# Moving SBUF-only products from VectorE to GpSimd in a two-layer codebook convolution

## The chip, the cores and the metric

The kernel runs on one core of one Trainium2 chip. The metric is the device time of one launch in microseconds, as the median of several runs. Engines are named as the profile does: PE is TensorE (PEld its weight loads), DVE is VectorE, ACT is ScalarE, POOL is GpSimd, and SP is SyncE, which here only issues DMAs.

## What is computed

The input `x` is 16 images of 256 channels, 28 x 28. Each is group-normalized (32 groups). Then come two layers of the same kind, a convolution through codebooks, and a closing gate:

```python
patches = 3x3 patches of each channel               # 9 values per channel and position
d       = |p|^2 - 2 p.centroids + |centroids|^2      # 16 centroids per channel
attn    = softmax(-d)
out     = sum over channels of attn @ (centroids @ w_sub)
# layer 1: relu(bn1(amm(gn(x)))) ; layer 2: bn2(amm(...))
s   = sigmoid(relu(mean(out) @ w1 + b1) @ w2 + b2)
x + relu(out * s + gn(x))
```

All of it is in 32-bit floats.

## The kernel before

**Blocks.** One image of one layer is four blocks: two halves of the channels (`hh`) by two halves of the rows (`t`, 14 x 28 = 392 positions), in the order `BLOCKS`. A block has nine *stacks*, tiles of 128 x 392: stack `k` holds, for its channels, the softmax-weighted part of patch row `k`. The list `KO` gives the order 8, 4, 5, 6, 7, 0, 1, 2, 3.

**How a stack is made.** `patches` (line 306 on, SyncE's queue) loads the 3x3 patches of the image from DRAM. `logits` (line 323, PE) writes eight PSUM banks per half block, `exps` (line 335, ACT) turns them into exponentials. `num_b` (line 384, PE) sums the denominators together with stack 8; `split_b` and `join_b` (lines 395 to 407, ACT and DVE) separate them, and `recip_dve` (line 410) inverts. `spread` (line 420, DVE) shuffles that reciprocal to the rows of a stack, into `rb`. `num_a` (line 370, PE) makes the numerators of stacks 0 to 7. Stacks 0 to 3 are copied out of PSUM unscaled by ACT (`copy_a`, line 430) and scaled later in SBUF by DVE (`scale_q`, line 424), as is stack 8; stacks 4 to 7 are scaled by DVE as they leave PSUM (`scale_a`, line 436).

**Seven products for eight.** The four blocks meet four weight matrices in a Strassen-like scheme. `PRODUCTS` lists eight calls of `product` (line 444, PE), numbered 5 to 12 by their slot: numbers 6 and 7 are the two parts of one product, 6 with the first four stacks of `KO`, 7 with the other five. Between them GpSimd forms differences of blocks, stack by stack, in place (`mix`, line 450). The results leave PSUM by `acc_copy` (ACT, line 466) and `acc_add` (DVE, lines 472 and 474), and two sums of regions by `reg_add` (line 479).

**Around the image.** In layer 0 the result, after batch norm and ReLU (`norm_out`, ACT, line 486), lies in the two tiles `hpads[0]` and `hpads[1]`, one per half of the output channels, which all images share. `to_home2` (line 499) scatters each with two indirect DMAs (r = 0 and 1) on GpSimd's queue into `home2[b]`; the second waits until the first has landed. The next image's input is normalized by `gn_apply` (line 291, GpSimd) and written to `home1` by `to_home1` (line 302, GpSimd's queue). For half of layer 1's blocks one group of logits is shifted by its maximum first (`wide_copy`, `wide_turn`, `wide_sub`, `wide_back`, `wide_exp`: DVE transposes, a reduction, a subtraction on line 355, and back); the subtraction runs on DVE for block 0 and on GpSimd for block 1. Layer 1 ends an image with `se_hidden`, `se_gate`, `finish_gate` (ACT), `finish_norm` (DVE, line 701), `finish_relu` (ACT), `finish_add` (GpSimd, line 707) and `store`.

**The order.** It is written out by hand. `at(slot, sub, f, ...)` files a call under a pair; at the end all calls are issued in the order of these pairs, and every engine runs its own in that order. An image begins every eight slots, so its slots 8 to 12 are slots 0 to 4 of the next. Even slots hold logits, `num_b`, `num_a` and a product, odd slots logits, `num_a` and a product. PSUM is a ring of eight banks, so an instruction that opens a bank waits for what read it eight banks ago; in each slot the eighth bank of the logits is the one of the product before. "Slot s" below is the slot modulo eight.

**Buffers.** The stacks live in a pool of `NQ` tiles that a small planner hands out by the slots of first and last use (`homes`, `LAST`).

## Time and profile before

| | us |
|---|---|
| median of 3 runs | 3113.1 (3111.44 to 3119.77) |
| profiled execution, its own time | 3117.03 |
| its span, first to last instruction | 3115.6 |
| PE busy in the span | 2845.3 |
| DVE busy | 2383.1 |
| POOL busy | 1643.0 |
| ACT busy | 1405.2 |
| mean granted clock of PE | 0.953 of full |

How to read the rows that follow. A row of the busy times by stretch holds: the stretch, its length, then busy us and (x instructions) of PE, PEld, DVE, ACT and POOL, the granted PE clock, the busy share of the DMA engines, and GB/s. A row of the timeline holds: start, length, engine, line, operation, out<-in names, shape, count, and in brackets how long the engine had been idle and what ended that. A row of the groups holds the count, total busy us, the mean ns of one, then idle time before them and what ended it. A row of one line's instructions holds min/median/max ns.

### The profile page before, as it was taken

The page shows a single profiled execution, that of the slowest core. Times are in us where ns is not written, and L with a number is a line of the kernel's source. Part 1 is how long each engine was busy: PE and PEld are TensorE (multiplying, and loading weights), DVE is VectorE, ACT ScalarE, POOL GpSimd, SP SyncE. Part 2 cuts the span into 40 slices and gives each one's busy share as a digit, 9 for nine tenths or more (in the row PEclk, how much of TensorE's full clock was granted, in tenths as well). Part 3 has the DMA queues.
Part 4 walks back from the last instruction along what each step waited for, and adds up shares of the span by engine and source line. Part 5 has one row for each costly group of instructions (what it writes and reads, how often), then busy time and mean ns, then how long its engine had stood idle before and what let it go on. Part 6 is the DMA issues. An engine that isn't in the chain of part 4 may idle for free.

```text
span 3115.6 us, 89074 instructions
## 1 busy us (share of the span) xinstructions
PE 2845.3 (91%) x37072; PEld 1313.2 (42%) x37072; DVE 2383.1 (76%) x4698; ACT 1405.2 (45%) x3216; POOL 1643.0 (53%) x1482
## 2 busy tenths in 40 slices
PE   6988999889999999899999999999999999999997
PEld 2333444434444444444444444444444444444444
DVE  5777677777767677676788887888888888788786
ACT  3434433433444434444344555454555454555443
POOL 4455456534655456554555544555554556454555
PEclk9999999999999999999999999999999999999999
DMA  9465555554555545555465344444444444444441
GB/s 230 91 123 148 159 141 147 126 144 101 128 142 138 128 100 128 142 138 126 92 141 138 82 108 107 105 101 105 93 103 108 99 109 98 105 91 109 103 103 46
DMA packets 211818, 368.10 MB, mean 118 GB/s; under 512 B 29432, under 2 KB 186472, under 8 KB 211408
## 3 DMA queue, kind: packets, MB, share of 16 engines
q1 hardware_dynamic: 199856, 300.39, 43.2%
...
q14 instruction: 114, 0.93, 0.1%
HBM read 284.78 MB, written 77.44 MB: 116 GB/s over the span
## 4 chain that ended last, share of the span: by engine, by line
PE 62%; DVE 28%; issue 3%; ACT 3%; DMA 2%; POOL 2%; SPq 0%; another core or an unknown queue 0%; DVEq 0%; POOLq 0%; ACTq 0%
PE acc L444 29%; PE lg L323 13%; PE nb L384 12%; DVE rb L420 7%; PE na L370 7%; DVE qs L424 6%; DVE r L410 5%; DVE y L701 2%; DVE qs L436 2%; ACT r L395 1%; DVE r L404 1%; DVE qs L407 1%; DVE hpad L472 1%; DMA home<-hpad,col 1%; POOL xpad L291 1%
## 5 line engine op out<-in xcount | busy, mean ns | idle before, releaser
L450 POOL TENSOR_TENSOR qs<-qs,qs 128x392 f32<-128x392 f32 x1152 | 1270.6, 1140 | 783.2 <-PE acc L444 621.6
L335 ACT ACTIVATE e<-lg 128x392 f32<-128x392 f32 x1920 | 782.1, 528 | 1051.1 <-PE lg L323 1049.0
L444 PE MATMUL acc<-qs,w_S 128*128 128x392 f32 x2304 | 822.1, 508 | 34.0 <-POOL qs L450 33.2
L323 PE MATMUL lg<-pt,wd 32*32 32x392 f32 x16384 | 637.6, 509 | 184.7 <-DVE hpad L472 85.1
L420 DVE STREAM_SHUFFLE rb<-r 128x392 f32<-128x392 f32 x1152 | 647.5, 595 | 0.0
L444 PEld LDWEIGHTS acc<-qs,w_S 128*128 128x128 f32 x2304 | 430.7, 193 | 428.3 <-POOL qs L450 85.0
L444 PE MATMUL acc<-qs,w_A 128*128 128x392 f32 x1728 | 595.5, 499 | 0.0
L424 DVE TENSOR_TENSOR qs<-qs,rb 128x392 f32<-128x392 f32 x640 | 537.3, 840 | 54.4 <-DVE rb L420 0.9
L323 PEld LDWEIGHTS lg<-pt,wd 32*32 32x32 f32 x16384 | 239.4, 104 | 510.8 <-issue 190.3
L444 PEld LDWEIGHTS acc<-qs,w_A 128*128 128x128 f32 x1728 | 321.5, 190 | 274.6 <-ACT e L335 39.6
L384 PE MATMUL nb<-e,cwb 64*32 64x392 f32 x8192 | 426.7, 557 | 0.2 <-issue 0.2
L370 PE MATMUL na<-e,cwa 64*32 64x392 f32 x8192 | 408.6, 497 | 14.0 <-DVE hpad L472 11.5
L404 DVE SCALAR_TENSOR_TENSOR r<-nb,kst,r 128x392 f32<-128x392 f32 x128 | 79.9, 624 | 414.0 <-ACT r L395 404.0
L410 DVE RECIPROCAL r<-r 128x392 f32<-128x392 f32 x128 | 331.9, 2593 | 0.0
L436 DVE TENSOR_TENSOR qs<-na,rb 128x392 f32<-128x392 f32 x512 | 252.7, 554 | 99.8 <-PE na L370 98.1
L384 PEld LDWEIGHTS nb<-e,cwb 64*32 64x32 f32 x8192 | 152.4, 118 | 268.8 <-issue 215.2
L499 POOL DMA_INDIRECT home<-hpad,col x60 | 60.4, 1006 | 370.2 <-ACT hpad L486 185.4
L370 PEld LDWEIGHTS na<-e,cwa 64*32 64x32 f32 x8192 | 143.7, 107 | 239.3 <-issue 111.1
L430 ACT COPY qs<-na 128x392 f32<-128x392 f32 x512 | 210.5, 505 | 12.9 <-PE na L370 12.7
L395 ACT ACTIVATE r<-nb,kst 128x392 f32<-128x392 f32 x128 | 86.7, 678 | 208.1 <-PE nb L384 186.0
L355 POOL TENSOR_TENSOR z<-z,mx 128x1568 f32<-128x1568 f32 x16 | 45.8, 2862 | 225.6 <-DVE mx L349 225.6
L341 ACT COPY e<-lg 128x392 f32<-128x392 f32 x128 | 52.9, 500 | 119.3 <-PE lg L323 119.3
...
## 6 DMA issues: line engine op xcount, KB each, us to landing
...
home<-xpad POOLq DMA_DIRECT2D x30, 899.0 KB, 7.0
...
home<-xpad SPq DMA_DIRECT2D x2, 899.0 KB
...
```

The lines of the kernel that those rows point to most:

```text
L323: nc.tensor.matmul(bk[32 * c : 32 * c + 32, :N].rearrange("p (r w) -> p r w", w=W), lhsT=wts["wd", u["hh"]][32 * i : 32 * i + 32, mm, c, : ...
L335: nc.scalar.activation(eg[:, i, :], bk[:, :N], AF.Exp, scale=2.0)
L370: nc.tensor.matmul(bs[r][32 * i : 32 * i + 32, :N], lhsT=wts["cwa", u["hh"]][64 * r : 64 * r + 64, mm, i, :], rhs=es[64 * r : 64 * r + 64, ...
L384: nc.tensor.matmul(bs[r][32 * i : 32 * i + 32, :N], lhsT=wts["cwb", u["hh"]][64 * r : 64 * r + 64, mm, i, :], rhs=es[64 * r : 64 * r + 64, ...
L395: nc.scalar.activation(r, b0[:, :N], AF.Identity, bias=zero, scale=m_hi)
L410: nc.vector.reciprocal(u["r"], u["r"])
L420: nc.vector.stream_shuffle(rb, u["r"], mask_of(k))
L424: nc.vector.tensor_mul(u["q", k], u["q", k], u.pop(("rb", k)))
L430: nc.scalar.copy(u["q", k], bk[:, :N])
L436: nc.vector.tensor_mul(u["q", k], bk[:, :N], u.pop(("rb", k)))
L444: nc.tensor.matmul(accs[key][:, :N], lhsT=wl[w][:, k, :], rhs=us["q", k], start=first and n == 0, stop=last and n == len(ks) - 1,)
L450: nc.gpsimd.tensor_tensor(out_u["q", k], in0["q", k], in1["q", k], ALU.subtract)
```

## The change

- **Pairs.** Stacks 0 to 7 are kept as pairs, tiles of 128 x 2 x 392 (14 of them), stack 8 in four single tiles. `mix` takes a pair in one instruction: five per difference instead of nine. `rb` is shuffled into pairs too, with one buffer of its own for stack 8.
- **Scaling.** `scale_q` moves from DVE to GpSimd: two pairs and one single per block.
- **Differences.** The second difference of layer 1 moves from slot 7, sub 2.6, to slot 8, sub 1.9. Product 6 takes three stacks and product 7 six.
- **Norm.** `gn_apply` moves to ACT, one slot later (slot 5, 0.9), and `to_home1` to SyncE's queue (slot 5, 1.9).
- **Scatters.** The four indirect DMAs of an image are filed at (12, 0.5), (12, 2.9), (13, 2.4) and (14, 2.9), one by one; before, they stood two and two at (12, 0.5) and (13, 0.5).
- **Sums.** The second `reg_add` moves from DVE to GpSimd and an `acc_add` more on DVE goes with it. All wide subtractions run on GpSimd.
- **Closing.** `finish_gate` and a `finish_norm` with a result of its own run on ACT in slot 14 (before: slot 15), `se_gate` ahead of `num_b`; a new `finish_sum` adds the two on GpSimd (on DVE for the last image); ReLU, add and store move up by half a slot to a slot.
- **Constants.** A mask of 512 columns becomes a row of 256 numbers and a comparison.

```diff
-NQ = 33
+NQ = {"pair": 14, "one": 4}
-    5: ("A11", 0, KO), 6: ("S1", 0, KO[:4]), 7: ("S1", 0, KO[4:]), 8: ("S3", 1, KO), 9: ("S4", 2, KO),
+    5: ("A11", 0, KO), 6: ("S1", 0, KO[:3]), 7: ("S1", 0, KO[3:]), 8: ("S3", 1, KO), 9: ("S4", 2, KO),
...
+    def gn_apply(b, k):
+        nc.scalar.activation(
+            grid(xpads[k])[:, 1 : H + 1, 1 : W + 1], xs[b][:, k].rearrange("p (r w) -> p r w", w=W), AF.Identity,
+            bias=nrm[:, b, 2, k : k + 1], scale=nrm[:, b, 1, k : k + 1],
+        )
...
+            rb = rpool.tile([P, 2, N], F32, tag="rb", name="rb", bufs=4)
+            for r in range(2):
+                nc.vector.stream_shuffle(rb[:, r, :], u["r"], mask_of(2 * mm + r))
...
-    def scale_q(u, k):
-        nc.vector.tensor_mul(u["q", k], u["q", k], u.pop(("rb", k)))
+    def scale_q(u, mm):
+        q = u["q", 8] if mm == 4 else pair(u, mm)
+        nc.gpsimd.tensor_tensor(q, q, u.pop(("rb", mm)), ALU.mult)
...
+            nc.gpsimd.tensor_tensor(pair(out_u, mm), pair(in0, mm), pair(in1, mm), ALU.subtract)
...
     def finish_gate(b, k):
-        nc.scalar.activation(y, y, AF.Identity, bias=nrm[:, b, 2, k : k + 1], scale=se[b][:, k : k + 1])
+        nc.scalar.activation(y, y, AF.Copy, scale=se[b][:, k : k + 1])
     def finish_norm(b, k):
-        nc.vector.scalar_tensor_tensor(y, xs[b][:, k], nrm[:, b, 1, k : k + 1], y, op0=ALU.mult, op1=ALU.add)
+        if k == 0:
+            ys[b, "t"] = io.tile([P, 1568], F32, tag="pb", name="xn")
+        nc.scalar.activation(
+            ys[b, "t"][:, HW * k : HW * k + HW], xs[b][:, k], AF.Identity,
+            bias=nrm[:, b, 2, k : k + 1], scale=nrm[:, b, 1, k : k + 1],
+        )
+    def finish_sum(b, k, eng):
+        eng.tensor_tensor(ys[b, k], ys[b, k], ys[b, "t"][:, HW * k : HW * k + HW], ALU.add)
...
+            for mm in (4, 2, 3, 0, 1):
+                at(g + 5, 2.5, mix, us[0], mm, us[1], us[0])
+                at(g + 7, 2.5, mix, us[1], mm, us[2], us[1])
+                at(g + (7 if l == 0 else 8), 2.6 if l == 0 else 1.9, mix, us[0], mm, us[2], us[0])
+                at(g + 10, 2.5, mix, us[0], mm, us[0], us[3])
...
-            at(g + 11, 0.02, reg_add, l, b, (1, 1), (1, 1), (1, 0), nc.vector)
+            at(g + 10, 0.05, reg_add, l, b, (1, 1), (1, 1), (1, 0), nc.gpsimd)
+            at(g + 11, 0.01, acc_add, l, b, 1, 1, (n, 10), pop=False)
+            at(g + 11, 0.02, acc_add, l, b, 0, 1, (n, 10))
...
-                        at(g + 12 + o, 0.5, to_home2, b, o)
+                        for r in range(2):
+                            at(g + 12 + o + (o and r), (0.5, 2.9)[r] if o == 0 else (2.4, 2.9)[r], to_home2, b, o, r)
...
-                        at(g + 4 if b else 3, 2.0 + 0.1 * q, gn_apply, b + 1, q)
-                        at(g + 4 if b else 3, 2.01 + 0.1 * q, to_home1, b + 1, q)
+                        at(g + 5 if b else 3, 0.9, gn_apply, b + 1, q)
+                        at(g + 5 if b else 3, 1.9, to_home1, b + 1, q)
...
-                at(g + 14, 2.1, se_gate, b)
+                at(g + 14, 1.05, se_gate, b)
                 for q in range(NB):
-                    at(g + 15, 0.9 + 0.01 * q, finish_gate, b, q)
-                    at(g + 15, 1.9 + 0.01 * q, finish_norm, b, q)
+                    at(g + 14, 1.9, finish_gate, b, q)
+                    at(g + 14, 1.91, finish_norm, b, q)
                     if b < B - 1:
-                        at(g + 16, 0.9, finish_relu, b, q)
-                        at(g + 16, 1.0, finish_add, b, q)
-                        at(g + 17, 0.6, store, b, q)
+                        at(g + 15, 0.5, finish_sum, b, q, nc.gpsimd)
+                        at(g + 15, 1.9, finish_relu, b, q)
+                        at(g + 16, 0.05, finish_add, b, q)
+                        at(g + 16, 2.9, store, b, q)
```

148 lines of the change are left out of this document (72 added, 76 removed).

## The prediction

> **What bounds the kernel now.** I read the page first (busy times, then the chain), then the busy time of each engine stretch by stretch, then the timeline of two images.
>
> ```profile
> PE 2845.3 (91%) x37072; PEld 1313.2 (42%) x37072; DVE 2383.1 (76%) x4698; ACT 1405.2 (45%) x3216; POOL 1643.0 (53%) x1482
> PE 62%; DVE 28%; issue 3%; ACT 3%; DMA 2%; POOL 2%; SPq 0%; another core or an unknown queue 0%; DVEq 0%; POOLq 0%; ACTq 0%
> ```
>
> TensorE is busy 91% of the time, yet the chain runs through VectorE for 28%. So TensorE stops for VectorE somewhere, and at most 270 us (3115.6 - 2845.3) of idle time is to be had, plus what a cold clock costs. The next two views locate it. Each row is one slot of the schedule. The first eight are one image of layer 0, slots 2, 3, 4, 5, 6, 7, 0, 1; the second eight are the same slots in layer 1.
>
> ```profile
> 840.64:853.54 12.90, 12.90 (x179) 6.00 (x178) 8.27 (x16) 6.00 (x14) 5.11 (x5) 1.00 0.35 76
> 853.54:864.28 10.74, 10.32 (x115) 4.80 (x115) 9.70 (x24) 4.41 (x10) 4.38 (x5) 1.00 0.42 91
> 864.28:877.88 13.60, 13.60 (x184) 6.58 (x183) 8.78 (x25) 6.59 (x15) 2.90 (x4) 1.00 0.47 126
> 877.88:887.52 9.64, 9.64 (x115) 4.74 (x114) 7.24 (x19) 3.81 (x9) 8.60 (x7) 1.00 0.66 201
> 887.52:900.53 13.01, 10.59 (x170) 4.79 (x169) 7.35 (x8) 6.49 (x15) 6.96 (x8) 0.87 0.73 231
> 900.53:907.48 6.95, 6.95 (x108) 3.17 (x107) 6.95 (x12) 3.72 (x9) 4.93 (x6) 1.00 0.48 94
> 907.48:927.71 20.23, 15.89 (x180) 6.43 (x179) 12.27 (x30) 6.12 (x14) 18.37 (x18) 0.83 0.46 104
> 927.71:937.36 9.65, 9.65 (x116) 4.75 (x115) 7.32 (x20) 3.23 (x8) 0.00 (x0) 1.00 0.48 102
> ```
>
> ```profile
> 2351.49:2363.68 12.19, 12.19 (x180) 5.94 (x179) 10.14 (x15) 6.01 (x14) 5.87 (x4) 1.00 0.63 180
> 2363.68:2374.45 10.77, 10.32 (x116) 4.77 (x115) 10.46 (x24) 5.99 (x13) 6.46 (x7) 1.00 0.42 91
> 2374.45:2387.20 12.75, 12.75 (x179) 5.99 (x178) 8.05 (x19) 6.68 (x16) 0.00 (x0) 1.00 0.36 77
> 2387.20:2397.13 9.93, 9.93 (x123) 5.01 (x122) 7.50 (x17) 3.90 (x10) 5.39 (x5) 1.00 0.49 99
> 2397.13:2406.56 9.43, 9.43 (x175) 4.55 (x173) 4.58 (x8) 6.62 (x16) 4.77 (x5) 1.00 0.47 106
> 2406.56:2413.57 7.01, 7.01 (x107) 3.23 (x106) 6.89 (x21) 5.85 (x13) 3.99 (x4) 1.00 0.48 101
> 2413.57:2433.93 20.36, 14.96 (x180) 6.18 (x179) 19.59 (x24) 7.62 (x16) 20.36 (x17) 0.83 0.28 62
> 2433.93:2443.96 10.03, 10.03 (x116) 4.77 (x115) 9.51 (x23) 4.61 (x9) 2.63 (x2) 1.00 0.53 142
> ```
>
> An even slot with a full product takes 12.19 us when nothing is late, an odd one 9.64. Slot 0 takes 20.23 and 20.36: 8 us are lost there in either layer, about 5 as a stop and 2.8 (14.96 - 12.19) because the granted clock falls to 0.83 around it. Layer 0 loses 3.6 more in slot 6. The images sum to 96.7 and 92.5 us. The timeline of slots 6, 7 and 0 says why.
>
> ```profile
> 897.52 6.73 DVE L424 TENSOR_TENSOR qs<-qs,rb 128x392 f32<-128x392 f32 x1
> 895.01 8.80 POOL L450 TENSOR_TENSOR qs<-qs,qs 128x392 f32<-128x392 f32 x9
> 913.76 1.53 PE L323 MATMUL lg<-pt,wd 32*32 32x392 f32 x8 [4.34 <-DVE hpad L472]
> L424 DVE TENSOR_TENSOR qs<-qs,rb x640: 566/568/9437, 52.3 to 3086.6; 128x392 f32<-128x392 f32 x160
> ```
>
> One scaling product (`scale_q`, line 424), 0.57 us in the median, takes 6.73 while GpSimd runs nine differences (`mix`, line 450) without a pause, and ends as they end. VectorE comes to the accumulator add (line 472) late, the add frees the eighth PSUM bank, and TensorE's logits stop for it. The Trainium skill (SBUF — State Buffer, Who interferes with whom) gives VectorE and GpSimd one exclusive port pair that a VectorE instruction with two SBUF inputs also needs; the 6.73 us agrees, though it outlasts one instruction.
>
> **The change, part by part.**
>
> ```profile
> L450 POOL TENSOR_TENSOR qs<-qs,qs 128x392 f32<-128x392 f32 x1152 | 1270.6, 1140 | 783.2 <-PE acc L444 621.6 <-DVE qs L424 109.6 <-DVE qs L436 51.6
> L707 POOL TENSOR_TENSOR y<-y,xt 128x784 f32<-128x784 f32 x30 | 60.0, 2020 | 0.0
> L355 POOL TENSOR_TENSOR z<-z,mx 128x1568 f32<-128x1568 f32 x16 | 45.8, 2862 | 225.6 <-DVE mx L349 225.6
> 880.81 1.98 DVE L436 TENSOR_TENSOR qs<-na,rb 128x392 f32<-128x392 f32 x4 [1.98 <-PE na L370]
> ```
>
> *GpSimd's products.* A pair has 784 elements: between 1.7 (an estimate: half of line 355's 2.86 is 1.43, a fifth more since its second operand is broadcast) and 2.28 us (twice the mean of 1.140). I take 2.0, the row of that shape (2.020); a single one is 0.98 (8.80/9). Per image GpSimd gets 8 pairs and 4 singles of scaling (20 us) and has 16 pairs and 4 singles of differences (36): 56 of about 92 us. It has room on average; what counts is the order of its queue. The stop in slot 0 goes, 8 us per image, since VectorE keeps no large instruction with two SBUF inputs: `scale_a` reads one from PSUM and takes 1.98 for four.
> By the Trainium skill (GPSIMD Engine Reference, 3.1 Elementwise), this is the wrong engine for elementwise work, VectorE being about twice as fast; 0.98 against 0.57 us for one stack agrees roughly. Its 4497 ns for 2048 elements would make a pair 1.72 us, an estimate by that page, and the sum below some 105 us lower; the measured row decides.
>
> *Where the stall goes: layer 0, slot 7.* The scatters' last one (o=1, r=1) now stands at slot 6, sub 2.9, behind `mix` and behind the scaling of stack 8. The next image's `acc_copy` at (slot 7, 0.0) overwrites the same `hpads[1]`, so it waits for that DMA to land. Behind it in ScalarE's queue stand the eight exponentials, whose banks TensorE's `na` products need.
>
> ```profile
> 879.83 1.64 PE L370 MATMUL na<-e,cwa 64*32 64x392 f32 x32
> 886.90 1.08 POOL L499 DMA_INDIRECT home<-hpad,col  x1 [0.31 <-issue]
> DMA to landing us min/median/max: 3.2/5.3/8.2
> 896.89 0.59 DVE L420 STREAM_SHUFFLE rb<-r 128x392 f32<-128x392 f32 x1
> 900.63 0.49 ACT L466 COPY hpad<-acc 128x392 f32<-128x392 f32 x1 [5.42 <-PE acc L444]
> 892.14 1.52 PE L370 MATMUL na<-e,cwa 64*32 64x392 f32 x32
> 3059.06 3.56 PE L444 MATMUL acc<-qs,w_S 128*128 128x392 f32 x10
> ```
>
> In this image's times: VectorE ends `scale_a` at 882.8; two shuffles of 0.59 give the first pair at 884.0. GpSimd then has two scalings to 888.0, the scatter r=0 to 889.1, five differences (0.98 + 4 x 2.0) to 898.1, stack 8's scaling (its shuffle ends 897.5) to 899.1, the scatter's issue to 900.2. It lands 5.3 later (the median of the landing row, which is of line 499's scatters), 905.5; `acc_copy` takes 0.49, and the first exponential, of the same shape, as much: 906.5. TensorE: `na` of slot 6 ends at 893.7, three stacks at 0.69 (ten matmuls, five stacks, take 3.56 less 0.1 of drain) take it to 895.7, and `na` of slot 7 could start 1.95 later (877.88 to 879.83), 897.7. Wait: about 9 us (7 to 12 by the landing's extremes), and I charge the 2.8 us of cold clock. The Trainium skill (TensorE: Matmul & The Clock Gate, What's actually happening) halves the clock after an idle window of some 3.4 us; the 0.83 rows, behind stops of 4 and 5 us, agree.
>
> Layer 0 by slots, 0 to 7: 12.2 + 2.8 cold + 0.7 (after slot 7's `na` the last pair of `mix` is ready at 2.5 + 4.0 + 0.98 + 8.0 = 15.5, wanted at 4.1 for product 7's six stacks + 6.0 of slot 0 before its product + 4.8 = 14.9) = 15.7; 9.65; 12.9; 11.2 (a third accumulator add before the bank is free, +0.5); 13.6; 9.64; 8.2 (9.43 less 0.69 for a stack and 0.6 for the gate's products, which layer 0 lacks); 6.95 + 0.69 + 9.0 = 16.6. Sum 97.5 against 96.7: +0.8, times 14 images: **+11**. In slot 6 the first three stacks' differences are ready by 892.1, ahead of product 6 at 893.7. The first two image boundaries have no such scatter; their slot 0:
>
> ```profile
> 93.67:116.03 22.36, 17.13 (x179) 6.29 (x178) 14.91 (x34) 6.54 (x14) 19.07 (x18) 0.77 0.42 99
> 197.82:222.40 24.58, 15.10 (x179) 6.47 (x178) 21.43 (x37) 6.22 (x14) 18.97 (x17) 0.79 0.41 90
> ```
>
> 22.36 and 24.58 become 13.0: **-21**.
>
> *Layer 1.* Gate and norm, four passes over 784 elements, move ahead of slot 7's exponentials. They begin as the copies end:
>
> ```profile
> 2403.18 1.64 ACT L430 COPY qs<-na 128x392 f32<-128x392 f32 x4
> 2435.42 1.81 DVE L359 STREAM_TRANSPOSE e<-z 128x1568 f32<-128x1568 f32 x1
> 2410.58 2.03 ACT L697 ACTIVATE y<-y,nrm,se_gt 128x784 f32<-128x784 f32 x2
> ```
>
> 2404.8, +0.6 for the gate's products now ahead of `nb`, +4 passes of about 1.0: 2409.4, `acc_copy` to 2409.9, first exponential 2410.4; `na` could have started at 2407.9. Wait 2.5. On GpSimd the closing adds (2 x 2.0) and the wide subtraction (2.9, now always there) stand behind five differences: from the end of `na` in slot 7, 2.5 + 4.0 + 9.0 + 4.0 + 1.0 + 2.9 = 23.4. VectorE, held at its transpose back, frees slot 2's last bank after that transpose (1.81), `scale_a` (1.98), four shuffles (2.4, less overlap) and an add of some 0.5: 29.8. Wanted at 4.1 + 12.2 + 0.7 + 9.64 + 1.7 = 28.3: 1.5 lost. Slots 0 to 7: 12.9, 10.0, 13.7, 11.8, 12.75, 9.93, 8.7, 10.2 = 90.0 against 92.5: -2.5, times 16: **-40**.
>
> *Ends.* In the last image few logits cover GpSimd:
>
> ```profile
> 3098.16 0.25 PE L670 MATMUL sep<-ysum,w_sb 128*16 128x1 f32 x4
> ```
>
> From `na` of the last slot 7, GpSimd needs the 20.5 us above without the subtraction, 1.0 for stack 8, 9.0, 4.0, 1.0 and 9.0 for the differences of product 12: 44.5, and TensorE ends 1.4 later, 45.9, where it took 39.1 (3059.1 to 3098.2): +6.8. ScalarE's two extra passes add 2, the first image's norm 1: **+10**.
>
> *At no cost.*
>
> ```profile
> home<-xpad POOLq DMA_DIRECT2D x30, 899.0 KB, 7.0
> ```
>
> The norm of the next image on ScalarE (2 passes, about 2 us) lies in slot 5, where ScalarE is busy 3.81 of 9.64; uncovered it would cost 2 us an image. Its two writes go from GpSimd's queue to SyncE's, ahead of the patches; by the row above they land 7.0 us after issue, so near 892, and the patches are wanted in slot 0, after 903. If that cover went they would be late next, by some 3 us. The single `rb1` buffer makes a shuffle wait for GpSimd's scaling of two slots before, some 20 us old. GpSimd's adds of regions replace VectorE's 16 per layer in slots where it has room. The constants' load shrinks, ahead of the first slot.
>
> Sum: 11 - 21 - 40 + 10 = -40, on the profiled execution's 3117.0 us (its span 3115.6 and 1.4 around it): 3077. It ran 3.9 above the median of 3113.1, so **3073**.
>
> **Rivals.**
> *A, GpSimd's queue is shorter than summed.* Each 0.1 us on a pair costs some 1.2 us per image (six pairs ahead of the scatter, six ahead of product 8 or the wide subtraction), 30 images and the tail: 37 us in all. Pairs at 1.8, a landing 1 us sooner (14 images) and half the cold clock (1.4 x 14) take off 74 + 14 + 20 = 108: **2965**. For it: a landing of 3.2 occurs, and 1.7 is the lower bound of a pair. Against: 2.020 is a measured mean, and the writes of the next image's norm share the DMA engines with this scatter. Patches late by 3 us would give 42 back.
> *B, GpSimd's queue is the bound: slower.* The same two places, by the same 37 us for each 0.1. It decides from 2.11 us a pair; at 2.28 it gives 3073 + 0.28 x 370 = **3177**. For it: the mean of 1.140 for half a pair. Against: that mean holds the times in which VectorE contended.
> *C, no change*: ScalarE's closing block in front of the exponentials costs 5 us, not 2.5: 2.5 x 16 = +40, **3113**. Against: ScalarE is 4.58 to 7.6 us busy a slot.
>
> **How the numbers follow.** Forecast 0.50 (own range 3030 to 3125), A 0.22, B 0.20, C 0.08. About 9 us (0.3%) can be told from no change here. Faster: 0.84 of the forecast plus A, 0.64; same: 0.05 + 0.08, 0.13; slower: 0.03 + 0.20, 0.23. A range of 2940 to 3160 reaches past A's time and most of B's.
>
> **What would show it.** Slot 0 near 13 to 16 us in both layers with no scaling product on VectorE; line 466 in layer 0 waiting some 9 us for the `home` DMA in slot 7; differences of 784 elements near 2.0; slot 7 of layer 1 at 10 us, with `acc_copy` behind the passes. The forecast falls if layer 0's slot 7 stays under 10 us, or if products in slot 0 wait over 3 us for GpSimd.

## Result and the profile after

The changed kernel takes 2994.6 us (median; 2993.3 to 2995.2), the kernel before 3112.3 beside it: a ratio of 0.962, 95% interval 0.960 to 0.964. That is 118 us less, where 40 were forecast. The direction was right, the size was not.

First the page of the changed kernel: busy times, then the chain.

```profile
PE 2797.5 (94%) x37072; PEld 1312.9 (44%) x37072; DVE 1791.3 (60%) x4010; ACT 1459.0 (49%) x3280; POOL 2044.7 (68%) x1372
PE 76%; POOL 8%; DVE 5%; ACT 4%; issue 3%; DMA 3%; SPq 0%; DVEq 0%; ACTq 0%; POOLq 0%
```

VectorE's share of the chain went from 28% to 5%, GpSimd's from 2% to 8%. The stretches by slot of the same two images as before follow: layer 0 (slots 2, 3, 4, 6, 7, 0), then layer 1 (slots 2, 3, 4, 6, 7, 0). Columns: window and length, busy time and instructions of PE, PEld, DVE, ACT, POOL, granted clock, DMA share, GB/s.

```profile
822.34:834.53 12.19, 12.19 (x179) 5.94 (x179) 6.89 (x15) 6.01 (x14) 4.61 (x5) 1.00 0.38 81
834.53:844.76 10.23, 10.23 (x116) 4.80 (x115) 6.66 (x18) 4.41 (x10) 10.23 (x6) 1.00 0.45 96
844.76:857.78 13.02, 13.02 (x184) 6.82 (x183) 7.52 (x20) 6.60 (x15) 4.66 (x8) 1.00 0.41 112
...
867.42:876.55 9.13, 9.13 (x167) 3.88 (x166) 2.62 (x4) 6.61 (x15) 8.94 (x7) 1.00 0.87 273
876.55:892.54 15.99, 11.02 (x109) 4.20 (x108) 7.79 (x23) 3.61 (x9) 5.29 (x5) 0.79 0.49 118
892.54:904.73 12.19, 12.19 (x179) 5.94 (x179) 6.90 (x15) 6.01 (x14) 12.19 (x8) 1.00 0.60 130
...
2256.73:2269.93 13.20, 12.96 (x179) 6.00 (x178) 12.04 (x24) 6.01 (x14) 13.20 (x8) 1.00 0.48 120
2269.93:2280.06 10.13, 10.13 (x115) 4.77 (x114) 7.26 (x16) 5.99 (x13) 10.13 (x7) 1.00 0.49 95
2280.06:2292.25 12.19, 12.19 (x179) 5.94 (x178) 6.88 (x15) 6.69 (x16) 3.12 (x3) 1.00 0.38 82
...
2302.18:2310.95 8.77, 8.77 (x174) 4.17 (x171) 4.26 (x6) 7.46 (x19) 8.12 (x5) 1.00 0.50 108
2310.95:2322.49 11.54, 10.05 (x109) 4.23 (x109) 8.09 (x23) 7.97 (x15) 7.46 (x5) 0.85 0.37 90
2322.49:2334.68 12.19, 12.19 (x180) 5.94 (x179) 9.99 (x17) 6.01 (x14) 12.19 (x8) 1.00 0.39 93
```

Slot 0 is clean in both layers: 12.19 us, where it was 20.23 and 20.36. The stop now lies in slot 7, at 15.99 us and a clock of 0.79 in layer 0, at 11.54 and 0.85 in layer 1. The timeline of the changed kernel shows what releases TensorE there (start, duration, engine, line; in brackets the idle time before and its releaser).

```profile
877.77 0.60 DVE L423 STREAM_SHUFFLE rb<-r 128x392 f32<-128x392 f32 x1
878.45 1.01 POOL L435 TENSOR_TENSOR qo<-qo,rb 128x392 f32<-128x392 f32 x1 [1.10 <-DVE rb L423]
879.62 1.01 POOL L511 DMA_INDIRECT home<-hpad,col  x1
882.91 0.49 ACT L479 COPY hpad<-acc 128x392 f32<-128x392 f32 x1 [6.90 <-issue]
883.45 1.53 PE L325 MATMUL lg<-pt,wd 32*32 32x392 f32 x8 [4.97 <-ACT hpad L479]
884.91 2.87 PE L372 MATMUL na<-e,cwa 64*32 64x392 f32 x32
...
2310.26 1.83 ACT L710 ACTIVATE y<-y,se_gt 128x784 f32<-128x784 f32 x2
2311.95 1.99 ACT L715 ACTIVATE xn<-xt,nrm 128x784 f32<-128x784 f32 x2
2313.82 0.50 ACT L479 COPY y<-acc 128x392 f32<-128x392 f32 x1
2314.37 0.86 PE L325 MATMUL lg<-pt,wd 32*32 32x392 f32 x8 [1.49 <-ACT y L479]
DMA to landing us min/median/max: 3.2/3.8/8.0
```

In layer 0 `acc_copy` (line 479) starts at 882.91, 3.3 us after the issue of the last scatter (line 511) began, and TensorE's logits wait 4.97 us for it; the 32 `na` matmuls that follow take 2.87 us instead of 1.5 to 1.6. (The last row is the time from the start of the issue to the landing, over all scatters of line 511.) The copy's row says "issue" where the scatter's landing is meant. In slot 7 of images 3 to 16 the trace puts this wait down to the scatter nine times and to "issue" five times, with 6.9 us in each of the five; the run with a second buffer (below) takes all fourteen away. The other waits of line 479 put down to "issue", some 50 us, are mostly of 3.1 us in slot 6; they stay in that run, and no matmul waits for them. In layer 1 the copy stands behind the four closing passes. Groups of the changed kernel (busy, mean ns, then idle time before them by releaser):

```profile
L463 POOL TENSOR_TENSOR qp<-qp,qp 128x784 f32<-128x784 f32 x512 | 939.5, 1867 | 0.0
L435 POOL TENSOR_TENSOR qp<-qp,rb 128x784 f32<-128x784 f32 x256 | 471.0, 1862 | 442.0 <-DVE rb L427 432.6 <-ACT xpad L293 5.3 <-ACT e L337 3.9
L361 DVE STREAM_TRANSPOSE e<-z 128x1568 f32<-128x1568 f32 x32 | 57.8, 1806 | 66.4 <-POOL z L357 66.4
L704 DVE TENSOR_SCALAR se_gt<-se_gt 128x2 f32<-128x2 f32 x16 | 27.8, 1739 | 113.7 <-ACT se_gt L701 113.7
L479 ACT COPY hpad<-acc 128x392 f32<-128x392 f32 x32 | 15.6, 488 | 165.9 <-issue 84.6 <-DMA home<-hpad,col 70.0 <-PE acc L454 11.2
```

A pair costs GpSimd 1.87 us, and GpSimd waits 433 us for VectorE's shuffles (line 427): its scaling is not late for lack of GpSimd's time.

Where the 124 us between the two profiled spans lie, from the starts of the slots: the first three images lose 13; images 4 to 16 of layer 0 gain 59; layer 1 gains 91; the last slot and what follows it lose 13 (60.0 us before, 73.3 after).

### The profile page after: what moved, and what is told of

Read it like the earlier page. It is cut to its first block, busy times and chain, and to the rows that moved or that the text cites. A ratio compares the mean times of both kernels' runs of the same rounds, so it can differ in the third digit from the quotient of the medians.

```text
span 2991.8 us, 88053 instructions
## 1 busy us (share of the span) xinstructions
PE 2797.5 (94%) x37072; PEld 1312.9 (44%) x37072; DVE 1791.3 (60%) x4010; ACT 1459.0 (49%) x3280; POOL 2044.7 (68%) x1372
## 4 chain that ended last, share of the span: by engine, by line
PE 76%; POOL 8%; DVE 5%; ACT 4%; issue 3%; DMA 3%; SPq 0%; DVEq 0%; ACTq 0%; POOLq 0%
PE acc L454 38%; PE lg L325 15%; PE na L372 11%; PE nb L386 11%; POOL qp L463 4%; DMA pt<-home 1%; DVE rb L427 1%; DMA home<-hpad,col 1%; ACT xn L715 1%; POOL qp L435 1%; ACT y L710 1%; POOL y L729 1%; DVE r L412 1%; POOL z L357 1%; ACT qp L440 1%
## 5 line engine op out<-in xcount | busy, mean ns | idle before, releaser
L463 POOL TENSOR_TENSOR qp<-qp,qp 128x784 f32<-128x784 f32 x512 | 939.5, 1867 | 0.0
L435 POOL TENSOR_TENSOR qp<-qp,rb 128x784 f32<-128x784 f32 x256 | 471.0, 1862 | 442.0 <-DVE rb L427 432.6
L454 PE MATMUL acc<-qp,w_S 128*128 128x392 f32 x2048 | 723.1, 504 | 0.9 <-POOL qp L463 0.9
L454 PEld LDWEIGHTS acc<-qp,w_S 128*128 128x128 f32 x2048 | 396.5, 195 | 324.2 <-issue 45.4
L454 PE MATMUL acc<-qp,w_A 128*128 128x392 f32 x1536 | 521.8, 492 | 0.4 <-POOL qp L463 0.4
L446 DVE TENSOR_TENSOR qp<-na,rb 128x392 f32<-128x392 f32 x512 | 255.9, 557 | 265.8 <-PE na L372 263.8
L454 PEld LDWEIGHTS acc<-qp,w_A 128*128 128x128 f32 x1536 | 291.7, 190 | 214.9 <-POOL qp L463 1.9
L435 POOL TENSOR_TENSOR qo<-qo,rb 128x392 f32<-128x392 f32 x128 | 130.5, 1020 | 353.3 <-DVE rb L423 353.2
L440 ACT COPY qp<-na 128x392 f32<-128x392 f32 x512 | 210.9, 504 | 26.8 <-PE na L372 24.5
L397 ACT ACTIVATE r<-nb,kst 128x392 f32<-128x392 f32 x128 | 86.9, 679 | 125.5 <-PE nb L386 120.4
L461 POOL TENSOR_TENSOR qo<-qo,qo 128x392 f32<-128x392 f32 x128 | 132.5, 1035 | 0.5
```

Of the source, the lines that this page charges most:

```text
L435: nc.gpsimd.tensor_tensor(q, q, u.pop(("rb", mm)), ALU.mult)
L440: nc.scalar.copy(u["q", 2 * mm + r], bk[:, :N])
L446: nc.vector.tensor_mul(u["q", 2 * mm + r], bk[:, :N], rb[:, r, :])
L454: nc.tensor.matmul(accs[key][:, :N], lhsT=wl[w][:, k, :], rhs=us["q", k], start=first and n == 0, stop=last and n == len(ks) - 1,)
L461: nc.gpsimd.tensor_tensor(out_u["q", 8], in0["q", 8], in1["q", 8], ALU.subtract)
L463: nc.gpsimd.tensor_tensor(pair(out_u, mm), pair(in0, mm), pair(in1, mm), ALU.subtract)
```

## Experiments

The table holds every run: its median, the ratio to the kernel before on the same chip, and the mean us of an image (images 9 to 16 of layer 0, images 2 to 15 of layer 1). A slot's time below is the median over these images.

| run | us | ratio (95%) | image, layer 0 | image, layer 1 |
|---|---|---|---|---|
| before | 3112.3 | 1 | 96.5 | 92.4 |
| after | 2994.6 | 0.962 (0.960 to 0.964) | 92.1 | 86.7 |
| after, scaling on VectorE | 3090.4 | 0.993 (0.992 to 0.995) | 92.6 | 92.8 |
| after, one stack each | 2997.3 | 0.963 (0.961 to 0.965) | 92.1 | 87.0 |
| after, closing norm in slot 5 | 2963.7 | 0.952 (0.950 to 0.953) | 92.1 | 84.7 |
| after, second buffer | 2888.2 | 0.928 (0.927 to 0.930) | 84.2 | 86.7 |
| after, 3 reciprocal buffers | 2993.3 | 0.962 (0.960 to 0.963) | 92.1 | 86.9 |
| after, both waits removed | 2841.4 | 0.913 (0.910 to 0.916) | 83.4 | 84.6 |
| after, norm on GpSimd | 3082.7 | 0.991 (0.988 to 0.994) | 98.5 | 86.7 |
| after, scatters together | 2927.8 | 0.939 (0.936 to 0.942) | 87.4 | 86.7 |
| after, closing as before | 3012.8 | 0.967 (0.965 to 0.970) | 92.1 | 87.9 |
| after, differences in slot 7 | 3143.9 | 1.010 (1.008 to 1.012) | 92.1 | 97.0 |
| before, scaling on GpSimd | 3122.5 | 1.003 (1.001 to 1.004) | 95.7 | 92.0 |
| before, norm and scatters | 3118.6 | 1.002 (1.001 to 1.003) | 95.2 | 92.6 |
| before, scaling, norm, scatters | 3097.4 | 0.995 (0.993 to 0.997) | 92.5 | 93.2 |
| closing norm, scatter earlier | 2937.5 | 0.943 (0.939 to 0.946) | 90.4 | 84.7 |
| closing norm, scatters in slot 5 | 2924.3 | 0.939 (0.936 to 0.941) | 88.6 | 84.7 |
| the same, adds later | 2905.9 | 0.933 (0.930 to 0.935) | 88.7 | 83.5 |
| second buffer, norm, adds later | 2836.7 | 0.912 (0.910 to 0.913) | 84.2 | 83.4 |
| the same, differences in slot 8 | 2825.3 | 0.907 (0.906 to 0.909) | 83.9 | 83.4 |

### Is it GpSimd's time for a pair that sets the end?

The prediction priced each 0.1 us on a pair at 37 us. One stack per instruction changes that price, and how long GpSimd holds up some small VectorE operations (last section).

```diff
-        nc.gpsimd.tensor_tensor(q, q, u.pop(("rb", mm)), ALU.mult)
+        for r in range(2):
+            nc.gpsimd.tensor_tensor(q[:, r, :], q[:, r, :], rb[:, r, :], ALU.mult)
```

The same is done in `mix`.

> The changed kernel, with GpSimd's differences and scaling products issued one stack at a time (two instructions for a pair). It measures what the pairing itself is worth. Two singles cost about 2 x 1.03 = 2.06 against 1.87 us for a pair. Theory of the prediction (GpSimd's queue decides slot 7 of layer 0 and slot 2 of layer 1; 37 us of time for each 0.1 us on a pair): +0.19 x 370 = about +70, some 3065. Rival (the queue has slack where the changed kernel's trace shows TensorE waiting: slot 7 waits for a landing that was issued by a chain of TensorE and VectorE, not by GpSimd's backlog): under +20, below 3015.

Its group of differences:

```profile
L470 POOL TENSOR_TENSOR qp<-qp,qp 128x392 f32<-128x392 f32 x1024 | 1010.8, 1025 | 0.0
```

Two stacks now cost 2 x 1.025 = 2.05 us, 0.18 more than a pair. By the slope that is +67; measured +2.7, within the spread of the two. In the profiled executions the first three images gain 4.7 us (slot 16, where the small operations stand, falls by 6.7), and the rest loses 8: still far from 67. The slope is refuted. The timeline above says why: the last scatter goes out behind the scaling of stack 8, which waits 1.10 us for a shuffle; GpSimd had ended its differences before. By that idle time a pair may cost about 2 us before it matters there (an estimate: 1.10 us over the six pairs ahead, 0.18 each).

### Is the wait on the scatter what slot 7 of layer 0 costs?

```diff
+    hodd = const.tile([P, NPAD], F32, name="hodd")
+    def hnow(b, o):
+        return hodd if o == 1 and b % 2 == 1 else hpads[o]
-            rb = rpool.tile([P, 2, N], F32, tag="rb", name="rb", bufs=4)
+            rb = rpool.tile([P, 2, N], F32, tag="rb", name="rb", bufs=3)
```

`hnow(b, o)` stands for `hpads[o]` in `region` and `to_home2`.

> The changed kernel, with a second buffer for the padded feature map of output half 1 (odd images use it), so that the accumulator copy of the next image no longer overwrites what the last scatter still reads; to make room, the two-stack buffers of shuffled reciprocals go from 4 to 3. Theory (the wait on the scatter's landing is what slot 7 of layer 0 costs): slot 7 of layer 0 falls from 16.3 to about 8 us, slot 0 and 6 unchanged, and 13 images x 8 = -105 us, some 2890. Rival (the wait only hides another one, GpSimd's queue: the differences of product 7 come late, or the buffers of reciprocals now do): slot 7 or 0 keeps most of it, under -40 us.

2888.2, -106. Slot 7 falls from 16.33 to 7.61, and line 483, the copy, no longer waits for a scatter:

```profile
827.07:834.68 7.61, 7.61 (x109) 3.55 (x108) 7.49 (x23) 3.71 (x9) 3.57 (x4) 1.00 0.76 180
L483 ACT COPY hpad<-acc 128x392 f32<-128x392 f32 x24 | 11.7, 488 | 61.6 <-issue 49.9 <-PE acc L455 11.8
```

The first row is slot 7 of the same image as above, without a stop and at a clock of 1.00; the 49.9 us in the second are those of slot 6. So the stop cost 8.7 us an image, 8.4 (15.99 less 7.61) in this one. There the copy started 6.25 us later in its slot than here (882.91 - 876.55 against 0.11); the rest, some 2 us, is the lower clock: `na` takes 1.3 us longer and the product 0.7. Slot 0 grew from 12.19 to 12.77: the 0.7 us for late differences, which the prediction put there, is real (TensorE waits there for line 464, `mix`) and was hidden by the longer stop. The fewer reciprocal buffers had no part in it:

```diff
-            rb = rpool.tile([P, 2, N], F32, tag="rb", name="rb", bufs=4)
+            rb = rpool.tile([P, 2, N], F32, tag="rb", name="rb", bufs=3)
```

> The changed kernel with 3 instead of 4 two-stack buffers of shuffled reciprocals, nothing else: it measures what the room for the second buffer cost by itself. Theory (the buffers have slack: slot 0 of layer 0 grew by 0.6 us in the run with the second buffer because product 7's last differences are late, not because of these): within 6 us of 2994.6. Rival (a shuffle waits for a free buffer): +8 us or more.

2993.3 against 2994.6: no difference.

### Do ScalarE's closing passes set slot 7 of layer 1?

```diff
-                    at(g + 14, 1.91, finish_norm, b, q)
+                    at(g + 13, 0.9, finish_norm, b, q)
```

> The changed kernel, with the closing norm passes (layer 1, two of the four passes on ScalarE in front of slot 7's exponentials) moved to slot 5, where x has been loaded and ScalarE has room. Theory: slot 7 of layer 1 is longer than its work because the accumulator copy and the exponentials stand behind four passes (1.83 for two gate passes, 1.99 for two norm passes): slot 7 falls from 11.5 to about 9.5 (2.0 less for the passes, plus some cold clock), so 14 to 15 images x 2 to 3 us = -30 to -45 us. Rival (slot 7 is set by the gate's products, whose vector arrives late, so the order of passes matters little): under -10 us.

2963.7, -31. Slot 7 falls from 11.47 to 8.10: two passes, 1.99 us together, were worth 3.4, the stop and its clock. But slot 2 grows from 12.57 to 13.58, as GpSimd's queue, which ends in the wide subtraction, is late next.

> The changed kernel with both: the second buffer for the padded feature map of half 1 (reciprocal buffers 4 to 3) and the closing norm passes moved to slot 5. Theory (two separate waits of ScalarE, one in each layer): the gains add, 2994.6 - 31 (norm alone) - 106 (buffer alone) = 2858. Rival (with both waits gone, GpSimd's queue is the next bound and gives part back): 2880 or more.

Second buffer and this edit together give 2841.4, 16 better than the sum of the two gains. 14 x 0.57 = 8 of these are in slot 6 of layer 0 (8.24 instead of 8.81, in the 64 logits matmuls); why these are faster in some of the kernels was not found.

### What is each part worth?

First the scaling, put back on VectorE.

```diff
-        nc.gpsimd.tensor_tensor(q, q, u.pop(("rb", mm)), ALU.mult)
+        nc.vector.tensor_tensor(q, q, u.pop(("rb", mm)), ALU.mult)
```

> The changed kernel, with the scaling products back on VectorE (two stacks per instruction); all else stays. Theory (starvation): a scaling product with two SBUF operands beside a run of GpSimd differences does not end before the run. Expected: scaling products of 784 elements with maxima of 7 to 10 us, slot 0 back near 18 to 20 us in both layers, and a time between the two kernels or above, 3080 to 3150. Rival (most of the 118 us comes from the other parts: norm on ScalarE, closing passes off VectorE, region adds): the time stays under 3020 and slot 0 under 14.

```profile
L435 DVE TENSOR_TENSOR qp<-qp,rb x256: 974/1412/7057, 55.6 to 3046.3; 128x784 f32<-128x784 f32 x128
```

3090.4: the scaling's place is worth 96 us here. The products are held up again (minimum 0.97, median 1.41, maximum 7.06 us), but slot 0 is 13.9 and 14.5, not 18 to 20. In layer 0 slots 1 to 3 are longer again, 10.02, 12.41 and 10.44, and in layer 1 slot 3 is 13.74. Then the scaling alone, in the kernel before:

```diff
-        nc.vector.tensor_mul(u["q", k], u["q", k], u.pop(("rb", k)))
+        nc.gpsimd.tensor_tensor(u["q", k], u["q", k], u.pop(("rb", k)), ALU.mult)
```

> The kernel before with one part of the change: the scaling products on GpSimd, one stack per instruction; nothing else. Theory (the prediction's first step: VectorE's starved scaling product is the loss of slot 0, and the scaling on GpSimd removes it in whichever surroundings): slot 0 falls from 20 to 12 to 14 us in both layers, less any delay of GpSimd's longer queue; the time lies 80 to 150 below 3113, some 3000. Rival (the move pays only together with the norm and the closing passes that left GpSimd and VectorE): GpSimd, which here still normalises and VectorE still holds products with two SBUF operands, delays the differences, and the time stays above 3070.

3122.5, nothing gained. Slot 0 of layer 0 does fall, from 19.4 to 12.3, and slots 1, 3 and 4 to 9.64, 9.69 and 13.02. But slot 6 rises from 13.3 to 18.0 and slot 2 from 12.9 to 16.7. In layer 1 slot 0 falls only from 20.4 to 16.4, and slot 2 rises from 12.2 to 18.1. Its timeline, slots 5 and 6 of layer 0:

```profile
879.62 3.01 POOL L291 TENSOR_SCALAR xpad<-xt,nrm 128x784 f32<-128x784 f32 x1
...
888.08 1.07 POOL L499 DMA_INDIRECT home<-hpad,col  x1 [0.31 <-issue]
894.30 0.98 POOL L499 DMA_INDIRECT home<-hpad,col  x1 [5.14 <-DMA home<-hpad,col]
895.31 3.92 POOL L424 TENSOR_TENSOR qs<-qs,rb 128x392 f32<-128x392 f32 x4
899.19 8.80 POOL L450 TENSOR_TENSOR qs<-qs,qs 128x392 f32<-128x392 f32 x9
...
900.25 4.69 PE L444 MATMUL acc<-qs,w_S 128*128 128x392 f32 x8 [7.28 <-POOL qs L450]
```

GpSimd spends two norm passes of 3 us, then stands 5.14 us between two scatters: the second is issued only when the first has landed (the row's releaser is the first one's DMA). The moved scaling, the differences and product 6 queue up behind, and TensorE waits 7.28 us. So scaling, norm and scatters together were tried in the kernel before, and norm and scatters without the scaling:

```diff
-        (eng or nc.gpsimd).tensor_scalar(
+        nc.scalar.activation(
...
-                        at(g + 12 + o, 0.5, to_home2, b, o)
+                        for r in range(2):
+                            at(g + 12 + o + (o and r), (0.5, 2.9)[r] if o == 0 else (2.4, 2.9)[r], to_home2, b, o, r)
```

> The kernel before with three parts of the change: scaling on GpSimd (one stack each), the next image's norm on ScalarE with its writes on SyncE's queue, and the scatters spread out; products, differences and closing passes as before. Theory (these parts need one another: with the scaling alone on GpSimd, its queue in slot 5 of layer 0 holds 6 us of norm passes and stands 5.14 us between two scatters, since the second is issued once the first has landed; product 6 then waits 7.28 us for the differences): layer 0's slot 6 falls from 18 to about 9.5, slot 2 from 16.7 to about 12.5, slot 7 grows by the wait on the last scatter to about 16; layer 0's images from 95.7 to 91 to 93, layer 1 stays at 92: 3050 to 3080. Rival (the pairing and the new order of the differences are what pays, so these parts give nothing in layer 0 either): within 15 us of 3122.

> The kernel before with the norm on ScalarE and the scatters spread, the scaling left on VectorE. Theory (the starved scaling in slot 0 stays, in both layers, and the relief of GpSimd only moves where it falls; the wait on the last scatter is new): slot 0 near 20, slot 6 at 9 to 10 instead of 13.3, slot 7 at 10 to 16; layer 1 unchanged at 92.4; 3090 to 3140. Rival (norm and scatters carry the gain by themselves): under 3060.

With all three layer 0's image is 92.5, within 0.4 of the changed kernel's; slot 6 falls from 18.0 to 9.24, slot 7 rises to 14.75. Without the scaling it is 95.2. In layer 0 the gain belongs to these parts together, and the theory holds, but for slot 2, which stays at 14.0 instead of 12.5. The time, 3097.4, lies above the range given: by the starts of the slots the first three images lose 13 us, one image of layer 1 another 13 and the last slot with its tail 12. Layer 1 gains nothing (93.2), so its gain in the changed kernel comes from elsewhere.

The norm alone, put back on GpSimd in the changed kernel with its old place and queue:

```diff
-        nc.scalar.activation(
+        nc.gpsimd.tensor_scalar(
...
-                        at(g + 5 if b else 3, 0.9, gn_apply, b + 1, q)
-                        at(g + 5 if b else 3, 1.9, to_home1, b + 1, q)
+                        at(g + 4 if b else 3, 2.0 + 0.1 * q, gn_apply, b + 1, q)
+                        at(g + 4 if b else 3, 2.01 + 0.1 * q, to_home1, b + 1, q)
```

> The changed kernel with the norm of the next image back on GpSimd and its two writes back on GpSimd's queue, at the place they had in the kernel before. Theory (the norm on ScalarE is covered and costs nothing in the running images, but the earlier and faster writes slow the landings of the last scatter or the fetch of instructions in the first images): slot 14 loses its 7 us stop, the first three images take about 10 us less; running images of layer 0 keep 92 us; 2980 to 2995. Rival (GpSimd has no room for it: two passes of some 2 us each come ahead of the scatters and of the differences): layer 0's images grow by 2 to 5 us, 3020 to 3070.

```profile
L293 POOL TENSOR_SCALAR xpad<-xt,nrm 128x784 f32<-128x784 f32 x32 | 96.9, 3029 | 0.0
L479 ACT COPY hpad<-acc 128x392 f32<-128x392 f32 x32 | 15.6, 488 | 279.0 <-DMA home<-hpad,col 223.3 <-issue 39.6 <-PE acc L454 10.7
```

3082.7, +88, more than the rival gave. Slot 6 grows from 8.9 to 16.4, as its `acc_copy` now waits too, for the second scatter of half 0. Behind the two passes this scatter goes out in slot 5 instead of slot 4, and with the two writes issued on the same queue just before it, it lands 7 to 10 us after its issue instead of 3 to 4 (images 10 to 15). What the passes and the writes cost by themselves was not separated. The stop in slot 14 of the first images stayed (16.5 us), so the norm's earlier writes do not make it.

### What makes layer 1's gain?

```diff
-                at(g + (7 if l == 0 else 8), 2.6 if l == 0 else 1.9, mix, us[0], mm, us[2], us[0])
+                at(g + 7, 2.6, mix, us[0], mm, us[2], us[0])
```

> The changed kernel with layer 1's second set of differences (nine stacks, for the product of S2) back in slot 7, as in the kernel before and in layer 0. Theory (in layer 1 GpSimd's run of 18 differences, 19.2 us with the scaling alone moved, is what then holds the next scaling, and with it VectorE's shuffles and the wide subtraction; the move behind slot 0's subtraction takes this away): slot 0 or slot 2 of layer 1 grows by 2 to 5 us, 15 images: 3025 to 3070. Rival (the buffers for eight stacks and the pairs give room enough): within 10 us of 2994.6.

3143.9: this one line is worth 149 us, and without it the changed kernel is slower than the one before. Slot 2 of layer 1 is 23.6 instead of 12.6. The timeline, slots 0 to 2:

```profile
2402.00 7.33 POOL L463 TENSOR_TENSOR qp<-qp,qp 128x784 f32<-128x784 f32 x4
...
2410.26 7.31 POOL L463 TENSOR_TENSOR qp<-qp,qp 128x784 f32<-128x784 f32 x4
2417.54 3.62 POOL L729 TENSOR_TENSOR y<-y,xt 128x784 f32<-128x784 f32 x2
...
2422.10 2.85 POOL L357 TENSOR_TENSOR z<-z,mx 128x1568 f32<-128x1568 f32 x1
...
2424.99 1.81 DVE L361 STREAM_TRANSPOSE e<-z 128x1568 f32<-128x1568 f32 x1 [11.58 <-POOL z L357]
...
2427.30 2.95 PE L325 MATMUL lg<-pt,wd 32*32 32x392 f32 x32 [4.19 <-DVE qp L446]
```

Two sets of differences and the adds (2402.0 to 2421.2, 19 us) stand ahead of the wide subtraction; VectorE waits 11.58 us at its transpose back, and behind that stand `scale_a` and the adds that free TensorE's banks. In the changed kernel the same wait is 66.4 / 16 = 4.15 us and TensorE hardly sees it. The forecast named this queue; it charged 1.5 us for it in slot 2, and 0.4 came.

The closing passes themselves were put back as well.

```diff
-        nc.scalar.activation(y, y, AF.Copy, scale=se[b][:, k : k + 1])
+        nc.scalar.activation(y, y, AF.Identity, bias=nrm[:, b, 2, k : k + 1], scale=se[b][:, k : k + 1])
...
+        nc.vector.scalar_tensor_tensor(y, xs[b][:, k], nrm[:, b, 1, k : k + 1], y, op0=ALU.mult, op1=ALU.add)
```

The schedule of gate, norm, relu, add and store is that of the kernel before.

> The changed kernel with layer 1's closing passes as the kernel before had them: gate with its bias on ScalarE behind slot 7's exponentials, the norm's multiply-add of 784 elements on VectorE (both operands in SBUF), relu and add in the next slot 0. Theory (the product of two SBUF operands left on VectorE is starved by GpSimd's differences, as the scaling was): layer 1's slot 0 grows by 3 to 8 us, slot 7 falls from 11.5 to about 8: images of 86.7 become 87 to 91, time 2995 to 3060. Rival (ScalarE's four passes in front of the exponentials cost more than the starved product): layer 1's images fall to 83 to 85 and the time to 2940 to 2970.

3012.8, +18: slot 0 of layer 1 rises from 12.19 to 17.4, slot 7 falls from 11.47 to 7.67. The changed closing is worth 1.1 us an image: 5.2 won in slot 0, 3.8 paid in slot 7 and 0.4 in slot 2.

### Where should the scatters stand?

```diff
-                            at(g + 12 + o + (o and r), (0.5, 2.9)[r] if o == 0 else (2.4, 2.9)[r], to_home2, b, o, r)
+                            at(g + 12 + o, 0.5, to_home2, b, o, r)
```

> The changed kernel with the scatters filed where the kernel before has them: both rows of half 0 at slot 4, sub 0.5, both of half 1 at slot 5, sub 0.5. Theory (the spreading puts the last scatter right ahead of the copy that overwrites what it reads): without it slot 7 of layer 0 falls from 16.3 to about 8, but GpSimd stands at slot 5 for the normalised rows ahead of its pairs of scaling: 13 images x 6 to 8.5 = -80 to -110, some 2885 to 2915. Rival (the spreading pays, since two scatters in a row hold GpSimd and the transfers land later): at or above 2995.

2927.8, -67: less than expected. Slot 7 falls to 7.7, but slot 6 grows from 8.9 to 11.7 as GpSimd stands between the scatters and the differences come late. The next runs start from the closing norm in slot 5 (2963.7). One issues the last scatter ahead of stack 8's scaling:

```diff
-                            at(g + 12 + o + (o and r), (0.5, 2.9)[r] if o == 0 else (2.4, 2.9)[r], to_home2, b, o, r)
+                            at(g + 12 + o + (o and r), (0.5, 2.9)[r] if o == 0 else (2.4, 0.5)[r], to_home2, b, o, r)
```

> The changed kernel with the closing norm passes moved to slot 5, and the last scatter (half 1, second row) issued ahead of stack 8's scaling of slot 6 instead of behind it; one buffer for the feature map, as in the changed kernel. Theory (in the changed kernel's trace the scatter is issued at 879.62, though GpSimd ends its differences at 877.35 and stands idle 1.10 before the scaling at 878.45): the landing comes 2.2 us sooner and slot 7 of layer 0 falls from 16.3 to about 14.1, part of the cold clock with it: 13 images x 2.2 to 3 = -29 to -39 on the norm's own 2964, some 2930. Rival (the landing takes longer where it meets the next image's writes, or the scatter was not what ended last): within 8 us of 2964.

2937.5, -26: slot 7 falls by 1.1, to 15.2, not by 2.2, and slot 6 by 0.6. The scatter goes out 1.5 us sooner in its slot, but lands 3.6 to 4.6 us after its issue instead of 3.2 to 3.3 (images 10 to 15): the rival holds in part. The other issues both of half 1 in slot 5:

```diff
-                            at(g + 12 + o + (o and r), (0.5, 2.9)[r] if o == 0 else (2.4, 2.9)[r], to_home2, b, o, r)
+                            at(g + 12 + o, (0.5, 2.9)[r] if o == 0 else (2.4, 2.45)[r], to_home2, b, o, r)
```

> The changed kernel with the closing norm passes in slot 5 and both scatters of half 1 one behind the other in slot 5, behind the scaling (sub 2.4 and 2.45); one buffer, reciprocal buffers 4 as in the changed kernel. Theory (the place of the last scatter alone makes the wait, the second buffer is not needed): slot 7 of layer 0 at about 7.6 and the time as with both waits removed, 2835 to 2850. Rival (a landing takes so long that one buffer still waits): slot 7 above 10 us, 2870 or more.

```profile
POOL home L511 <- DMA home<-hpad,col: 81.0, 18, 6.9
```

2924.3, not 2835 to 2850. Slot 7 is 8.28, as the theory has it, but GpSimd stands 81.0 / 18 = 4.5 us at the second scatter, and slot 6 is 13.3. Spreading the scatters out removes that stand and puts the last one in front of the copy; of what was tried, only a second buffer avoids both. On this run the two closing adds were moved:

```diff
-                        at(g + 16, 0.05, finish_add, b, q)
-                        at(g + 16, 2.9, store, b, q)
+                        at(g + 18, 2.0, finish_add, b, q)
+                        at(g + 18, 2.9, store, b, q)
...
-                at(g + 9, 2.6, load_x, b)
+                at(g + 11, 0.6, load_x, b)
```

> As the run before (closing norm in slot 5, both scatters of half 1 in slot 5), and the two closing adds of x on GpSimd (2 x 1.85 us) moved from the start of the next slot 0 to the end of slot 2, x's load of the next image to match. Theory (in layer 1, once the closing block no longer delays slot 7, GpSimd's queue decides slot 2: wide subtraction behind the differences and the adds; slot 2 is 13.58 there against 12.19 with nothing late): slot 2 falls by 1.0 to 1.4 and slot 0 by 0.3 in layer 1, 15 images x 1.3 to 1.7 = -20 to -25 us against the run before. Rival (the differences, not the adds, are ahead of it): within 8 us of the run before.

2905.9, -18: slot 2 of layer 1 falls from 13.58 to 12.19, slot 0 stays at 12.5. Close to what was expected.

### A faster version

> The changed kernel with the second buffer for the feature map (reciprocal buffers 4 to 3), the closing norm passes in slot 5 and the closing adds of x at the end of slot 2. Theory (three separate places, the gains add): 2841.4 less 15 images x 1.3 = about 2822, layer 1's slot 2 at 12.19. Rival (with a buffer more, the adds' new place delays something else): 2835 or more.

2836.7, not 2822: layer 1 gains its 1.2 us an image, but slot 6 of layer 0 is back at 8.81. With layer 0's second differences moved too:

```diff
-                at(g + (7 if l == 0 else 8), 2.6 if l == 0 else 1.9, mix, us[0], mm, us[2], us[0])
+                at(g + 8, 1.9, mix, us[0], mm, us[2], us[0])
```

> The run with the second buffer, the norm in slot 5 and the adds in slot 2, with layer 0's second set of differences moved to slot 8 as in layer 1. Theory (in layer 0 slot 0 is 12.77 because TensorE waits for differences of GpSimd, and this set stands in the same run): slot 0 of layer 0 falls to 12.2, 14 images x 0.5 = -7 us. Rival (the first set alone is late, and the second is wanted early in slot 2): no change, or slot 2 of layer 0 grows; within 4 us of 2836.7 or above.

The page of this run:

```profile
PE 2726.3 (96%) x37072; PEld 1295.3 (46%) x37072; DVE 1787.6 (63%) x4010; ACT 1462.8 (52%) x3280; POOL 2045.5 (72%) x1373
```

2825.3, the fastest of all: 0.907 of the kernel before. The theory fell: slot 0 of layer 0 stays at 12.77, so it is the first set that is late. About 8 of the 11 us come from one slot, slot 2 of the first image of layer 1, which the last differences of layer 0 no longer hold up (20.1 to 12.19).

## Why the prediction was right and wrong

Part by part, on the profiled executions: layer 0 from image 4 on gains 59 us where a loss of 11 was forecast, layer 1 gains 91 for 40, the first three images lose 13 for a gain of 21, the ends lose 13 for 10. The two layers are 121 us better than forecast, and 37 of these are hidden by luck, since the other two parts are worse.

Forecast and measured, us by slot 0 to 7 (medians as in the experiments):

| | 0 | 1 | 2 | 3 | 4 | 5 | 6 | 7 | sum |
|---|---|---|---|---|---|---|---|---|---|
| layer 0, forecast | 15.7 | 9.65 | 12.9 | 11.2 | 13.6 | 9.64 | 8.2 | 16.6 | 97.5 |
| layer 0, measured | 12.19 | 9.64 | 12.19 | 10.23 | 13.02 | 9.64 | 8.86 | 16.33 | 92.1 |
| layer 1, forecast | 12.9 | 10.0 | 13.7 | 11.8 | 12.75 | 9.93 | 8.7 | 10.2 | 90.0 |
| layer 1, measured | 12.19 | 9.58 | 12.57 | 10.17 | 12.19 | 9.93 | 8.77 | 11.47 | 86.9 |

**What held.** The stop of slot 0 goes. The stall moves to slot 7 of layer 0, where `acc_copy` waits for the last scatter; the slot's length was right to 0.3 us, though by two errors that cancel (next point), and the second buffer proves the cause. In layer 1 the copy stands behind the closing passes. A pair at 1.87 us lies between the two bounds, near the row chosen.

**Step that failed, layer 0: "12.2 + 2.8 cold + 0.7" for slot 0.** The wait in slot 7 was put at 9 us and the cold clock charged on top, in slot 0. Measured, the copy starts 6.25 us late. The scatter lands 3.3 us after its issue begins, where the prediction allowed 6.4: 1.1 for the issue and, behind it, 5.3 from the landing row. That row counts from the start of the issue (counted from its end, 880.63, even the shortest landing, 3.2, would come after the copy's start at 882.91), and 5.3 is the median over all scatters of the kernel before. The slow clock, some 2 us, falls into slot 7, right behind the stop, as the 0.79 row shows; slot 0 runs at 1.00. The 0.7 for late differences is covered by the longer slot 7; it shows (0.6) once that wait is gone. This term alone is 3.5 x 13 = 46 us.

**Step that failed, both layers: the values of slots 1 to 4 taken over from before.** 12.9, 11.2 and 13.6 in layer 0, and 10.0, 13.7, 11.8 and 12.75 in layer 1, are the old slots with additions. But the old ones held losses of VectorE's scaling. The run with the scaling alone on GpSimd shows slots 1, 3 and 4 at 9.64, 9.69 and 13.02 in layer 0, and 9.59, 9.64 and 12.19 in layer 1. The prediction let the gain of an unloaded VectorE appear in slot 0 only. Together with layer 0's slot 2 it is 2.3 us an image in layer 0, and 3.7 in layer 1 with the 1.1 us of slot 2 by which the wide subtraction's delay was overrated; 0.7 more comes in slot 0 there.

**Layer 1, slot 7.** 10.2 was forecast, 11.47 came. The wait of 2.5 was about right: `na` starts 4.2 us into the slot, and 1.95 with the closing as before. But in 12 of the 14 images the clock fell to 0.85, which was not charged. In the other two it stayed at 1.00 behind the same stop, and the slot took 9.95:

```profile
2225.01:2234.96 9.95, 8.46 (x110) 3.69 (x109) 7.98 (x23) 7.97 (x15) 6.35 (x4) 1.00 0.41 85
```

**Step that failed: the slope of 37 us for 0.1 us on a pair**, on which rivals A and B rest. The forecast added GpSimd's times as though it were always last. Its own sum had GpSimd at 898.1 and the shuffle at 897.5, 0.6 us apart; at 1.87 us a pair the shuffle comes last and the price no longer counts. The estimate by the Trainium skill (GPSIMD Engine Reference, 3.1 Elementwise), 1.72 us a pair and some 105 us below the sum, is not borne out: 1.87 was measured, and two stacks at 2.05 cost hardly more time. Rival A's time, 2965, is nearer the result than the forecast. Of its three terms the sooner landing and the smaller cold clock came; the price of a pair, 74 of its 108 us, did not. Rival B's mechanism is real under other conditions: with 18 stacks of differences in one run the kernel is slower than before. Rival C did not come.

**A gain the prediction did not list.** Norm and scatters were costed as moves that spare nothing. In the kernel before, GpSimd stood 134.5 us at scatters that waited for the previous one to land, as its waits show:

```profile
POOL home L499 <- DMA home<-hpad,col: 134.5, 23, 7.9
```

Norm on ScalarE and the spread scatters take some 11 us an image (two passes of 3 and a stand of 5.14) out of GpSimd's queue in slot 5. Without that the scaling's move pays nothing (3122.5).

**First images.** -21 was forecast for two slots 0. Slot 8 did fall from 22.4 to 15.9, but slot 16 rose from 24.6 to 27.7, slot 14 from 11.3 to 19.6, and slot 23 took its first scatter wait (20.0). Slot 16 holds the ranking of the channels, small VectorE operations beside the differences; three of the five in each half take 1.9 us instead of 1.1 (last section). In slot 14 the waits of TensorE show a stop put down to issue (the second row is from the page's list of DMA queues: packets, MB, share):

```profile
PE na L372 <- issue: 7.3, 2, 7.1
q8 instruction: 296, 4.85, 0.7%
```

Slot 14 is long in every variant (14 to 21 us, the kernel before 11.3). The trace gives a hint. The stop ends at 187.35, 1.4 us after a packet of queue q8 (185.9), and the packet before that one started 22 us earlier, where this queue moves one in 10 us on average. In 18 of the 20 runs the stop ends 1.1 to 1.5 us after such a packet. This points to TensorE's instructions arriving late; no run tests it, and why they would come later than before is open. **Ends:** +10 was forecast; the last slot and its tail grew by 13.
